# Causal attention in a macaron block: units of 32 queries with all sixteen heads for the maxima, the diagonal mask inside the product of the maxima, one summed tile for each query block

## The chip, the core and the metric

The kernel runs on one core of a Trainium2 chip. The metric is the device time of one launch in microseconds; the time before is the median of three runs. The engines are called PE (TensorE matmul), PEld (its weight loads), DVE (VectorE), ACT (ScalarE), POOL (GpSimd) and SP (SyncE, which here issues nearly all transfers).

## What is computed

The input x is 16 x 512 x 128 (batch elements, tokens, width), fp32. A feed-forward half step, causal attention and another feed-forward half step follow each other, each on a normalised input:

```python
x = x + 0.5 * ffn(layernorm(x))
x = x + attn(layernorm(x))
x = x + 0.5 * ffn(layernorm(x))

# ffn: w = simulate_quantize_int4(kernel)
#      x @ w + bias + (x @ a) @ b                      128 -> 128, rank 16
# attn, 16 heads of 64, latent of 32:
#      q = x Wq ; lat = x Wkv_down ; k = lat Wk_up ; v = lat Wv_up
#      attn = softmax(where(key <= query, q k / 8, lowest)) ; y = attn v ; y Wout
```

The kernel folds Wk_up into Wq and Wv_up into Wout, so that a head's query has 32 entries (LD) and keys and values are the latent itself, the same 32 rows for all heads.

## The kernel before

Scores are computed twice for each batch element. The first time queries lie on the partitions and keys along the free axis (`sx`, `s_parts`); DVE reduces them to the negated row maximum (`find_maxima`, L651 and L655, tile `nmax`). The second time keys lie on the partitions and queries along the free axis (`tx`, `t_parts`), the negated maximum is added by a small product, and ACT takes the exponential (`exponentials`, L664) into the probabilities `pt`. These are the moving operand of the product with the latent (`values`, tile `o`, L763) and of the product with ones for the row sums (`sums`, tile `s`, L763). All four groups of 32 partitions hold a copy of the 32 latent rows, one for each of four heads, so PE runs four products side by side, one on each group of 32 rows of its array (scores) or of 32 columns (values, sums, queries, projection).

The sixteen heads form four groups of four (`HG`, `NG`). Work goes through pairs of groups. A pair takes five steps, in each of which every head streams 512 score columns:

```python
STEP = ((0, 0), (1, 0), (2, 0), (1, 1), (0, 1))
T_BLOCKS = (((0, 0, 512, 0),), ((3, 384, 128, 0), (1, 128, 384, P)))
```

Kind 0 is query block 3 against all four key blocks for the maxima, and key block 0 against all queries for the probabilities; kind 1 joins query blocks 2 and 0 (key blocks 3 and 1); kind 2 is query block 1 (key block 2) for both groups of the pair. A batch element takes ten steps, the sixteen of them 160, n = 0 to 159.

In a step, `burst(n, s_at, t_at)` issues the score products of step n and the probability products of the step LAG = 6 earlier. `merge` (L641) interleaves the two streams of matmuls on PE. The maxima need the causal mask on the diagonal blocks: for each of four sub-blocks of 32 queries a bf16 product of `mask_w` and `eye2_b` adds -1e30 above the diagonal. The small product that brings the maxima takes them as three bf16 terms (`maxima`, L728 to L732 on POOL; turned by PE in `maxima_t`, tile `mt`; stored by ACT as `rows`), with `ones_u` as weights. It does not mask; after the exponential POOL zeroes the upper triangles of `pt` (`zeros`, L677).

For the row sums POOL first adds probability tiles of equal query range (`add_01`, L747; `add_2`, L752; `add_23`, L757), and PE then multiplies ones with three tiles of 128, 384 and 128 columns (`sum_products`). The sums go to DRAM one head at a time (L799), come back over 128 partitions (L801), DVE takes the reciprocal (L831), and this goes through DRAM again and is broadcast to the 32 partitions of each head (L833, L836, tile `rb`). POOL multiplies values and reciprocals (`normalise`, L839, tile `ot`), and PE projects (`yp`, L385).

Between the bursts stands the gap: values, sums, turned maxima of earlier steps, and parts of other batch elements. `plan` puts the parts of `front` (first feed-forward, normalisation, keys `kt_ps`, queries `qt_ps`) and `tail` (projection, second feed-forward `fp_c`) at fixed steps given by tuples such as FRONT_STEPS and TAIL_STEPS. Each engine runs its instructions in the order in which they are issued here; SP issues the transfers, in the same order. The reciprocal square root of the normalisation is refined by one Newton step of three DVE instructions on 12 columns (`ln_newton`, L344 to L346). Before step 0 the weights are prepared; after step 159 `late_burst` and the code behind it work off the six probability steps that remain.

The PSUM banks are two pools: four single banks (`bank`, for `tx` and the products in the gaps) and two pairs (`two_banks`, for `sx` and at times a third product of a gap).

Of the kernel before, what the change touches and what calls it, by code (L numbers as in the profile page):

```python
# [11 lines left out]
F32 = mybir.dt.float32  # L12
# [6 lines left out]
P = 128  # L19
# [6 lines left out]
def macaron_kernel(  # L26
# [24 lines left out]
    assert D == P and NT * P == L and L <= 512 and HG == 4 and H % HG == 0  # L51
    scale = HD**-0.5
# [4 lines left out]
    io = ctx.enter_context(tc.tile_pool(name="io", bufs=3))  # L57
# [54 lines left out]
    def load_heads(src, n, name):  # L112
        t = const.tile([P, NW, n], F32, tag=name, name=name)
        nc.sync.dma_start(t, src.rearrange("(t p) n -> p t n", p=P))
        return t

    wq_sb = load_heads(wq_t, D, "wq_sb")
    wk_sb = load_heads(wk_t, LD, "wk_sb")
    xs[1] = load_x(1)
    zs[1] = load_blocks(x[1], "a1")  # L120
    wv_sb = load_heads(wv_t, LD, "wv_sb")
    wo_sb = load_heads(wout, D, "wo_sb")
# [8 lines left out]
    terms = []  # L131
    for k in range(2):
        t3 = const.tile([P, NT, P], BF16, tag=f"terms{k}", name=f"terms{k}")
        nc.vector.memset(t3, 0.0)
        terms.append(t3)
    ones_u = const.tile([P, 2, P], BF16, tag="ones_u", name="ones_u")
# [6 lines left out]
    eye_b = const.tile([P, LD], BF16, tag="eye_b", name="eye_b")  # L143
    for h in range(HG):
        rows = slice(h * LD, (h + 1) * LD)
        nc.vector.tensor_copy(eye_b[rows, :], ident[rows, ts(h, LD)])
    eye2_b = const.tile([P, 2, LD], BF16, tag="eye2_b", name="eye2_b")
    for k in range(2):
        nc.vector.tensor_copy(eye2_b[:, k, :], eye_b)
    for u in range(2):  # L150
        pick = const.tile([P, 1], F32, tag=f"pick{u}", name=f"pick{u}")
        nc.vector.tensor_reduce(pick, ident.rearrange("p (h c) -> p c h", c=LD)[:, 3 * u : 3 * u + 3, :], AX.XY, ALU.max)
        nc.vector.tensor_scalar(ones_u[:, u, :], ones_f, pick, None, ALU.mult)


    mask_w = const.tile([P, NT, P], BF16, tag="mask_w", name="mask_w")
    nc.gpsimd.memset(mask_w, 0.0)

    def masks():
        for h in range(HG):  # L160
            rows = slice(h * LD, (h + 1) * LD)
            nc.gpsimd.affine_select(
                mask_w[rows, :, :], mask_w[rows, :, :], pattern=[[-LD, NT], [1, P]],
                compare_op=ALU.is_ge, fill=MASK, base=0, channel_multiplier=-1,
            )
# [175 lines left out]
    def ln_newton(ln, whats):  # L341

        y, e, r, var = columns(ln, whats)
        nc.vector.scalar_tensor_tensor(e, var, EPS, y, ALU.add, ALU.mult)  # L344
        nc.vector.scalar_tensor_tensor(e, e, -0.5, y, ALU.mult, ALU.mult)
        nc.vector.scalar_tensor_tensor(r, e, 1.5, y, ALU.add, ALU.mult)  # L346
# [4 lines left out]
    def ln_scale(src, name, ln):  # L351

        xn = act2.tile([P, NT, D], F32, tag="xn", name=f"xn_{name}")
        for t in range(NT):
            nc.scalar.activation(xn[:, t, :], src[:, t, :], AF.Copy, scale=rstd(ln, "b", t))  # L355
        return xn
# [7 lines left out]
    def turn_blocks(z, name, tag):  # L364
        xt = act2.tile([P, L], F32, tag=tag, name=f"{tag}_{name}")
        nc.vector.transpose(xt, z.rearrange("p n c -> p (n c)"))
        return xt

    def turn(src, name, tag):
# [3 lines left out]
        xt = act2.tile([P, L], F32, tag=tag, name=f"{tag}_{name}")  # L373
# [3 lines left out]
    def with_bias(src, name, engine):  # L377
        xb = act2.tile([P, NT, D], F32, tag="xb", name=f"xb_{name}")
# [10 lines left out]
    def ffn(xt, ln, xb, name, tag, bufs):  # L389


        return ffn_out(ffn_product(xt, name), ln, xb, name, tag, bufs)

# [6 lines left out]
    def ffn_out(fp, ln, xb, name, tag, bufs):  # L400
        dst = io.tile([P, NT, D], F32, tag=tag, name=f"{tag}_{name}", bufs=bufs)
# [16 lines left out]
    def normalised(w):  # L418
        whats = [k for k, b in (("c", w - 2), ("b", w + 2), ("a", w + 3)) if 0 <= b < (B - 2 if k == "c" else B)]
# [4 lines left out]
        ln_newton(lns[w], whats)  # L424
        yield

    def front(b, st):
# [23 lines left out]
        x1 = st["x1"] = ffn(xt, la, xb, na, "x1", 5)  # L451
# [11 lines left out]
        xnt = turn_blocks(z, nb, "xnt_b") if b else turn(xn, nb, "xnt_b")  # L463
        yield
        mp = take(f"kt_ps_{b}")
        kt = st["kt"] = act2.tile([P, L], F32, tag="kt", name=f"kt_{b}", bufs=3)
# [21 lines left out]
        def query(g):  # L488
            mp = take(f"qt_ps_{b}_{g}")
            product(mp, wqk_flat[:, ts(g, P)], xnt)  # L490
            if g % 2 == 0:
                st["qt", g] = act2.tile([P, 2, L], F32, tag="qt", name=f"qt_{b}_{g}", bufs=4)
            nc.scalar.copy(st["qt", g - g % 2][:, g % 2, :], mp)  # L493

        yield
        query(0)
        yield
        query(1)
        yield
        query(2)  # L500
        yield
        query(3)
        yield

    def latent(b, st):

        lat = st["lat"] = act2.tile([P, NT, LD], F32, tag="lat", name=f"lat_{b}", bufs=3)
# [7 lines left out]
    FRONT_STEPS = (-31, -30.5, -29, -28, -21, -19.25, -16, -16, -13, -10.5, -8, -4.25, -4, -3.5, -3.25, -2, 3, 4)  # L515
    SECOND_STEPS = (-9.5, -8.5, -7, -5.5, -5, -4.25, -4, -3.5, -3.25, -2, 3, 4)
    THIRD_STEPS = (-18.5, -18.5, -18.5, -18, -17.5, -17.25, -16, -16) + FRONT_STEPS[8:]
    FOURTH_STEPS = (-27, -26, -25.5, -25) + FRONT_STEPS[4:]
    TAIL_STEPS = (1.75, 2.5, 2.75, 3.5, 4.5, 7, 7, 7.75, 10.5)
    NORMALISED_STEPS = (5, 6)  # L520

    def tail(b, st, late=False):


        x2 = io.tile([P, NT, D], F32, tag="x2", name=f"x2_{b}")
        nm = f"c{b}"
        ln = ln_tile(nm) if late else ln_of("c", b)
        for half in (0, 1):
            yp = take(f"yp_{b}_{half}")[:, : 2 * D]
            for t in (0, 1):  # L530
                for g in range(NG):
                    product(yp[:, ts(t, D)], st["ot"][:, g, ts(2 * half + t, P)], wvo[:, g, :],
                            t == 0 and g == 0, g == NG - 1)
            nc.vector.tensor_tensor(
                x2[:, ts(half, 2), :], yp.rearrange("p (t d) -> p t d", d=D), st["x1"][:, ts(half, 2), :], ALU.add
            )
            if half and not late:
                there = to_dram(x2, nm)
            yield
            ln_stats(x2, ln, "c", (2 * half, 2 * half + 1))  # L540
            yield
        if late:
            ln_rstd(ln, "c")
            yield
            ln_newton(ln, "c")
            yield
            xt = turn(x2, nm, "xt_c")
        else:
            z = load_blocks(there, nm)
            yield  # L550
        xb = with_bias(x2, nm, nc.vector if late else nc.gpsimd)
        yield
        if not late:
            xt = turn_blocks(z, nm, "xt_c")
            yield
        fp = ffn_product(xt, nm)
        if late:
            yield
        x3 = ffn_out(fp, ln, xb, nm, "x3", 3)
        if not late:  # L560
            yield
# [4 lines left out]

    STEP = ((0, 0), (1, 0), (2, 0), (1, 1), (0, 1))

# [539 lines left out]
```

## Time and profile before

| what | value |
|---|---|
| runs | 810.03, 811.99, 812.89 us; median 811.99 |
| profiled execution | span 808.8 us (no separate time is listed for it) |
| PE | busy 786.1 us (97%), 15400 matmuls |
| PE weight loads | 507.6 us (63%) |
| POOL | 676.1 us (84%), 675 instructions |
| DVE | 620.9 us (77%), 1318 |
| ACT | 488.1 us (60%), 971 |
| mean granted TensorE clock | 0.995 |
| first score product, first probability product, last step's end | 30.28, 52.35, 767.76 us |
| chain that ended last | PE 70%, DVE 9%, POOL 6%, DMA 5%, ACT 5% |

A product in fp32 appears as two matmul instructions. The busy time of a group is the union of its instructions, so it is less than count times mean where four run side by side. A matmul's duration includes the time in which it drains, and so overlaps the next one's start; the time of a section on PE is better taken from its start to the next section's start. The steady part repeats every batch element, ten steps.

### The profile page before, as it was taken

To read this page: it belongs to the slowest core of one execution; us is meant where nothing else is said; L and a number is where in the kernel's file an instruction comes from. 1 tells how busy PE (TensorE), PEld (TensorE's weight loads), DVE (VectorE), ACT (ScalarE), POOL (GpSimd) and SP (SyncE) were. 2 spreads that over 40 slices of the span, in tenths; PEclk is the share of its full clock that TensorE was granted. 3 is DMA by queue.
4 is the path that set the end of the run, shared out by engine and by line. 5 is a ranking of instruction groups with operands and counts; after the bars stand their busy time and mean duration, and the time that the engine had idled before them with its cause. 6 is when DMAs were issued, how large, how long until landed. Compare 5 with 4: busy or idle time off the path is not lost.

```text
span 808.8 us, 35715 instructions
## 1 busy us (share of the span) xinstructions
PE 786.1 (97%) x15400; PEld 507.6 (63%) x15400; DVE 620.9 (77%) x1318; ACT 488.1 (60%) x971; POOL 676.1 (84%) x675
## 2 busy tenths in 40 slices
PE   7899999999999999999999999999999999999987
PEld 5556566675666667666666666666566666666644
DVE  7887886878878697877869787777978777686817
ACT  1237675657566675756657575666657666665661
POOL 1018989999988999989899898989989979998992
PEclk9989999999999999999999999999999999999999
DMA  5123122232422323332232423223223222211201
GB/s 138 28 57 68 32 69 68 65 72 73 95 61 70 80 62 83 74 83 60 70 89 55 93 63 82 69 61 93 51 53 77 58 63 66 70 44 47 58 24 48
DMA packets 171022, 54.01 MB, mean 67 GB/s; under 512 B 119512, under 2 KB 162680, under 8 KB 170864
## 3 DMA queue, kind: packets, MB, share of 16 engines
q1 hardware_dynamic: 170096, 51.44, 27.2%
q8 instruction: 120, 1.97, 1.0%
q10 hardware_dynamic: 768, 0.30, 0.1%
q14 instruction: 38, 0.31, 0.1%
HBM read 37.90 MB, written 13.80 MB: 64 GB/s over the span
## 4 chain that ended last, share of the span: by engine, by line
PE 70%; DVE 9%; POOL 6%; DMA 5%; ACT 5%; SPq 2%; issue 2%; DVEq 0%; POOLq 0%; ACTq 0%
PE sx L641 17%; PE o L763 14%; PE tx L641 13%; PE s L763 7%; PE qt_ps L385 6%; PE yp L385 6%; DVE nmax L651 3%; POOL b L747 3%; DMA rb<-recs 2%; PE fp_c L385 2%; ACT xn_b L355 2%; DMA recs<-rec 2%; PE fp_a L385 1%; POOL ot L839 1%; ACT pt L664 1%
## 5 line engine op out<-in xcount | busy, mean ns | idle before, releaser
L651 DVE TENSOR_REDUCE nmax<-sx 128x2 f32<-128x768 f32 (+2 forms) x384 | 312.6, 863 | 105.9 <-PE tx L641 67.6
L664 ACT ACTIVATE pt<-tx 128x512 f32<-128x512 f32 x616 | 319.5, 598 | 85.3 <-PE tx L641 78.8
L641 PE MATMUL sx<-kt,qt 32*128 32x512 f32 (+3 forms) x2048 | 324.4, 444 | 0.0
L641 PE MATMUL tx<-qt,kt 32*128 32x512 f32 x1728 | 319.3, 469 | 0.0
L747 POOL TENSOR_TENSOR b<-pt,pt 128x768 f32<-128x768 f32 x126 | 226.8, 1822 | 0.5
L641 PEld LDWEIGHTS sx<-kt,qt 32*128 32x128 f32 x2048 | 176.8, 186 | 24.7 <-issue 1.0
L677 POOL TENSOR_SCALAR_AFFINE_SELECT pt<-pt 128x1024 f32<-128x1024 f32 (+1 forms) x162 | 144.8, 900 | 17.2 <-ACT pt L664 15.4
L763 PE MATMUL o<-pt,lat 128*32 128x512 f32 x1984 | 146.4, 435 | 0.8 <-POOL pt L677 0.8
L641 PEld LDWEIGHTS tx<-qt,kt 32*128 32x128 f32 x1728 | 131.5, 185 | 5.1
L763 PEld LDWEIGHTS o<-pt,lat 128*32 128x32 f32 x1984 | 62.5, 109 | 77.9 <-issue 59.0
L641 PE MATMUL tx<-rows,ones_u 6*128 6x512 bf16 (+1 forms) x988 | 109.9, 297 | 1.1 <-DVE wvo L292 0.5
L839 POOL TENSOR_TENSOR ot<-osb,rb 128x512 f32<-128x512 f32 x62 | 79.0, 1275 | 35.9 <-DMA rb<-recs 33.6
L655 DVE TENSOR_REDUCE nmax<-sx 128x4 f32<-128x1024 f32 x64 | 75.4, 1219 | 31.9 <-PE tx L641 31.8
L782 ACT COPY osb<-o 128x512 f32<-128x512 f32 x62 | 36.3, 585 | 92.1 <-PE o L763 92.1
L641 PE MATMUL sx<-eye_b,mask_w 32*128 32x64 bf16 (+1 forms) x2560 | 87.8, 183 | 2.4 <-DVE nmax L655 1.7
L641 PEld LDWEIGHTS <-ones_u 6*128 6x128 bf16 x1024 | 43.1, 92 | 74.3 <-issue 61.6
L641 PEld LDWEIGHTS <-mask_w 32*128 32x128 bf16 x2560 | 67.4, 92 | 32.7 <-issue 24.6
L752 POOL TENSOR_TENSOR b<-b,pt 128x512 f32<-128x512 f32 x63 | 80.5, 1278 | 5.1
L757 POOL TENSOR_TENSOR b<-pt,pt 128x512 f32<-128x512 f32 x63 | 80.4, 1276 | 0.1
L385 PE MATMUL qt_ps<-xnt_b_b,wqk 128*32 128x512 f32 x512 | 68.0, 603 | 0.2
L763 PE MATMUL s<-b,ones_f 128*32 128x384 f32 x992 | 65.1, 380 | 3.1 <-POOL b L752 2.6
L493 ACT COPY qt<-qt_ps 128x512 f32<-128x512 f32 x64 | 37.5, 586 | 48.4 <-PE qt_ps L385 48.4
(194 smaller groups left out, 815.6 us busy)
## 6 DMA issues: line engine op xcount, KB each, us to landing
rb<-recs SPq DMA_DIRECT2D x248, 64.0 KB
x<-in_x_dram SPq DMA_DIRECT2D x16, 256.0 KB
sums<-ssb SPq DMA_DIRECT2D x248, 2.0 KB
z_a<-in_x_dram SPq DMA_DIRECT2D x60, 64.0 KB
blocks_b<-xn_b SPq DMA_DIRECT2D x15, 256.0 KB
z_b<-blocks_b SPq DMA_DIRECT2D x60, 64.0 KB
kt<-kt_d SPq DMA_DIRECT2D x60, 64.0 KB
out_dram<-x_c SPq DMA_DIRECT2D x15, 256.0 KB
```

The costliest lines, as they stand in the source:

```text
L385: nc.tensor.matmul(dst[ts(h, LD), :], lhsT=w[:, ts(h, LD)], rhs=mv, start=start, stop=stop, skip_group_check=True)
L493: nc.scalar.copy(st["qt", g - g % 2][:, g % 2, :], mp)
L641: nc.tensor.matmul(dst, lhsT=w, rhs=mv, start=first, stop=last, skip_group_check=True)
L651: nc.vector.tensor_reduce(nmax[:, i, heads, u], sx[:, :, col : col + (i + 1) * P], AX.X, ALU.max, negate=True)
L655: nc.vector.tensor_reduce(nmax[:, 1, heads, :], sx.rearrange("p k (u n) -> p k u n", u=2), AX.X, ALU.max, negate=True)
L664: nc.scalar.activation(pt[:, :, 2 * pair + k, :], tx[k].rearrange("p (b n) -> p b n", n=P), AF.Exp)
L677: nc.gpsimd.affine_select(diag, diag, pattern=[[0, diag.shape[1]], [1, P]], compare_op=ALU.is_ge, fill=0.0, base=0, channel_multiplier=-1,)
L747: nc.gpsimd.tensor_tensor(*flat, ALU.add)
L752: nc.gpsimd.tensor_tensor(b01, b01, st["pt", 2, g][:, u], ALU.add)
L757: nc.gpsimd.tensor_tensor(both, st["pt", 2, g][:, 2 + u], st["pt", 1, g + u][:, 0], ALU.add)
L763: nc.tensor.matmul(dst[ts(h, LD), :].rearrange("p (b n) -> p b n", n=P), lhsT=w[h] if isinstance(w, list) else w, rhs=mv, start=start, sto ...
L839: nc.gpsimd.tensor_tensor(turned(st)[:, g, :], st["osb", g], st["rb", g], ALU.mult)
```

## The change

The scores of a query are taken for all sixteen heads at once. `qt` now holds, for each of the four partition groups, query and head group interleaved (`(q g)`: 512 queries x 4 groups), so that 128 columns of it are 32 queries of four groups.

* For the maxima a unit is one or two blocks of 32 queries (`S_UNITS`), and a block's product ends at its own last key: block qb streams (qb + 1) x 32 key columns. The mask is one small product for each head and unit (`tri`, 32 columns wide, `eye4`).
* For the probabilities a unit is one pair of query block i and key block j <= i of 128 each (`T_UNITS`, ten pairs), 512 columns of (query, group) for each of the four partition groups.
* On the diagonal pairs the product of the maxima carries the mask as well. The turned maxima have 32 rows for each partition group, three of them the bf16 terms and 26 a one-hot of the query; the weights `diag_w` hold -1e30 for masked pairs. 128 queries are cut into five pieces of 26 (`SUB`, `SUBS`), so five small products of up to 104 columns stand in place of one of 512. `zeros` is gone.
* `nmax` is split into bf16 terms and turned three times an element instead of twice.
* For the row sums POOL adds whole tiles of 2048 columns (`add`, six an element) until one tile for each query block is left; PE multiplies ones with that one tile. Sums and reciprocals travel for two query blocks at a time: one transfer out, one back, one out, four broadcasts.
* Values of block i are i + 1 products of 512 columns. The copies of `qt`, `o` and `s` by ACT interleave or separate query and group.
* The Newton step of the planned normalisations runs on POOL as five instructions.
* LAG is 5. All four query products of the first element precede step 0, and the planned parts, the gaps and the end are laid out anew. Weights and a helper tile share the six `pt` buffers; several tiles have other buffer counts.

```diff
-    STEP = ((0, 0), (1, 0), (2, 0), (1, 1), (0, 1))
-    T_BLOCKS = (((0, 0, 512, 0),), ((3, 384, 128, 0), (1, 128, 384, P)))
+    S_UNITS = ((12,), (13,), (14,), (15,), (8, 3), (9, 2), (10, 1), (11, 0), (7, 4), (6, 5))
+    T_UNITS = ((3, 0), (3, 1), (3, 2), (3, 3), (2, 0), (2, 1), (2, 2), (0, 0), (1, 0), (1, 1))
...
+    def s_parts(sc, st, unit, pair, masks_last):
...
-        for s in range(NT):
-            for k in range(2):
-                rows = ts(2 * pair + k, LD)
-                small_.append((diag[:, k, :, ts(s, LD)], mask_w[rows, s, :],
-                               eye2_b[rows, : diag.shape[2], :], not masks_last and s == 0, masks_last))
...
+                small_.append((at, eye4[rows], tri[rows, : len(ends), :], not masks_last and m == 0, masks_last))
+        for n_, qb in enumerate(unit):
+            w, col = both[n_]
             for k in range(2):
                 rows = ts(2 * pair + k, LD)
+                large.append((sc[:, k, col : col + w], st["qt"][rows, ts(qb, P)], st["kt"][rows, :w],
+                              masks_last and n_ == 0, not masks_last))
...
+    def t_parts(tx, st, unit, pair, maxima_last=False):
+        i, j = unit
...
+            if i == j:
+                for m in range(SUBS):
+                    q = slice(m * SUB * NG, min((m + 1) * SUB, P) * NG)
+                    up = slice(r * LD, r * LD + LD)
+                    small_.append((tx[k][:, q], diag_w[up, int(i == 0), m, :], top[up, q], first and m == 0, maxima_last))
             else:
+                up = slice(r * LD, r * LD + 3)
+                small_.append((tx[k], ones_b[up, :], top[up], first, maxima_last))
+            large.append((tx[k], st["kt"][rows, ts(j, P)], st["qt"][rows, ts(i, L)], maxima_last, first))
...
-    def zeros(st, g, kind, u, heads=slice(0, 4)):
-        pt = st["pt", kind, g + (u if kind < 2 else 0)]
-        diag = pt[:, : (1 if kind == 0 else 2), heads].rearrange("p b k n -> p (b k) n")
-        nc.gpsimd.affine_select(
...
+    def add(st, i, one, two):
+        left, right = st["pt", i, one], st["pt", i, two]
+        if ("both", i, one) not in st:
+            st["both", i, one] = probs.tile([P, HG, L], F32, tag="both", name=f"both_{st['b']}_{i}{one}", bufs=3)
...
+        nc.gpsimd.tensor_tensor(st["both", i, one], left, right, ALU.add)
...
+    def values(st, i):
+        o_ps = take(f"o_{st['b']}_{i}")
+        for j in range(i + 1):
+            streamed(o_ps, st["lat"][:, j, :], st["pt", i, j], j == 0)
...
+        for k, w in enumerate(which):
+            s_ps = take(f"s_{b}_{w}")
+            streamed(s_ps, ones_f[:, :LD], st.get(("both", w, 0), st["pt", w, 0]), True)
+            nc.scalar.copy(*by_group(ssb[:, ts(k, L)], s_ps))
...
+    def ln_newton(ln, whats, engine):
+        if engine is nc.gpsimd:
+            engine.tensor_scalar(e, var, EPS, -0.5, ALU.add, ALU.mult)
+            engine.tensor_tensor(r, y, y, ALU.mult)
+            engine.tensor_tensor(e, e, r, ALU.mult)
+            engine.tensor_scalar(e, e, 1.5, None, ALU.add)
+            engine.tensor_tensor(r, e, y, ALU.mult)
...
+    FRONT_STEPS = (-28, -27, -26, -20, -19, -18, -17, -16.5, -11, -9.5, -7.5, -6.25, -6, -5)
+    QUERY_STEPS = (-5, -4, -3, -2)
+    TAIL_STEPS = (0, 1, 2, 3, 3.5, 5, 6, 7, 9)
+    NORMALISED_STEPS = (4, 4.5)
...
+    STEPS, LAG = len(S_UNITS), 5
...
+    GAPS = {
+        0: ((maxima_t, 2, 1),),
+        2: ((values, 2, 1),),
+        3: ((sums, (3, 0), 1), (values, 0, 1)),
+        4: ((maxima_t, 0, 0),),
+        5: ((values, 1, 1),),
+        6: ((sums, (2, 1), 1),),
+        8: ((maxima_t, 1, 0),),
+        9: ((values, 3, 0),),
+    }
+    RECIPROCALS = {5: (((3, 0), 1),), 8: (((2, 1), 1),)}
+    NORMALISED = {7: ((3, 1), (0, 1)), 9: ((2, 1), (1, 1))}
+    ADDED = {
+        7: ((3, 0, 1, 0),),
+        9: ((3, 2, 3, 0),),
+        0: ((3, 0, 2, 1),),
+        1: ((2, 0, 1, 1),),
+        3: ((2, 0, 2, 1),),
+        5: ((1, 0, 1, 1),),
+    }
+    TERMS = {3: 0, 7: 1, 9: 2}
```

In these tables the key is the step within an element, and the last number of an entry says how many elements back its work belongs. In a step POOL's instructions are issued in the order: add, split of the maxima (TERMS), products with the reciprocals (NORMALISED).

## The prediction

> **What bounds the kernel now.** The first view read was the windows view, busy time of each engine in stretches of one batch element (columns: stretch, length, then busy time and instructions of PE, PEld, DVE, ACT, POOL; granted clock, DMA share, GB/s):
>
> ```profile
> 463.36:510.30 46.94, 46.79 (x954) 30.36 (x953) 37.38 (x78) 30.13 (x61) 42.74 (x43) 1.00 0.31 71
> 510.30:557.34 47.04, 46.80 (x955) 30.36 (x953) 36.72 (x78) 30.15 (x61) 42.79 (x43) 1.00 0.33 76
> ```
>
> An element takes 47.0 us, PE is busy through all but 0.2 us of it at full clock, and POOL is second with 42.8. So the price of an edit is PE time, as long as POOL stays below PE. The next view is PE's timeline inside that element. It shows one burst, from 513.45 to 515.68, and two sections behind it:
>
> ```profile
> 513.45 0.39 PE L641 MATMUL tx<-rows,ones_u 6*128 6x512 bf16 x2
> 513.46 0.26 PE L641 MATMUL sx<-eye_b,mask_w 32*128 32x32 bf16 x8
> ...
> 515.40 0.25 PE L641 MATMUL sx<-eye_b,mask_w 32*128 32x32 bf16 x8
> 515.68 0.43 PE L763 MATMUL s<-pt,ones_f 128*32 128x128 f32 x8
> 515.93 1.05 PE L763 MATMUL s<-b,ones_f 128*32 128x384 f32 x16
> 516.79 0.41 PE L385 MATMUL mt<-ident_b,terms 128*32 128x128 bf16 x16
> 517.13 0.70 PE L641 MATMUL tx<-qt,kt 32*128 32x512 f32 x2
> ```
>
> Taking each section from its start to the next one's start, the element 510.30 to 557.34 is: ten bursts 22.65, values (o) 9.04, sums (s) 4.96, queries (qt_ps) 3.79, projection (yp) 3.54, the two feed-forward products 1.80, turned maxima (mt) 0.68, keys 0.39, idle 0.19; together 47.04. One of the four sums takes 1.54 instead of 1.11, and the chain of waits names what holds it:
>
> ```profile
> 544.13 3.55 POOL b L747 x2
> 547.69 0.07 issue
> 547.75 1.29 POOL b L752
> 549.04 0.04 issue
> 549.09 1.07 PE s L763 x16
> ```
>
> Last came the groups by form (busy time, mean ns of one), for the prices:
>
> ```profile
> L747 POOL TENSOR_TENSOR b<-pt,pt 128x768 f32<-128x768 f32 x126 | 226.8, 1822 | 0.5
> L651 DVE TENSOR_REDUCE nmax<-sx 128x2 f32<-128x1024 f32 x128 | 152.7, 1219 | 43.7 <-PE tx L641 42.1 <-PE sx L641 1.0
> L752 POOL TENSOR_TENSOR b<-b,pt 128x512 f32<-128x512 f32 x63 | 80.5, 1278 | 5.1
> L651 DVE TENSOR_REDUCE nmax<-sx 128x2 f32<-128x256 f32 x128 | 53.1, 415 | 0.0
> L345 DVE SCALAR_TENSOR_TENSOR e_w<-e_w,y_w 128x12 f32<-128x12 f32 x11 | 17.4, 1580 | 0.4
> L346 DVE SCALAR_TENSOR_TENSOR r_w<-e_w,y_w 128x12 f32<-128x12 f32 x11 | 4.4, 399 | 0.4
> ```
>
> **PE, part by part, per element.** Both kernels have ten steps an element.
>
> Score columns. Before, every row group streams 10 x 512 = 5120 columns for the maxima. After, the units are 416, 448, 480, 512 and six of 416 columns, 4352: 768 fewer. The values section prices a column, with four matmuls side by side: 9.04 us for 5120 columns, 1.77 ns; the sums give 1.11 us for 640, 1.73 ns. That is -1.3 us.
>
> Mask matmuls. A row group has 4 in a burst, then 1 (2560 to 640 in all). In the start-up, where no other work is mixed in, eight of them in two row groups hold the next product back by 0.12 us, 30 ns each:
>
> ```profile
> 32.82 0.29 PE L641 MATMUL sx<-eye_b,mask_w 32*128 32x64 bf16 x8 [0.26 <-DVE nmax L651]
> 32.94 1.12 PE L641 MATMUL sx<-kt,qt 32*128 32x384 f32 x8
> ```
>
> Three fewer by 0.03 by ten bursts is -0.9. The upper bound is the 0.28 us from 515.40 to 515.68: three quarters of it would be -2.1, but most of that time is the last products draining ahead of a section of another shape, which stays. I take -0.9.
>
> Sums. One stream of 512 columns in place of 128+384+128 = 640: 4 x 128 x 1.73 ns, rounded down for the start of each section, -0.75 (bounds -0.6 and -0.9).
>
> Values: the same columns in 10 streams instead of 16; between nothing and -0.3, I take -0.1.
>
> Turned maxima: three instead of two, one takes 517.13 - 516.79 = 0.34, so +0.34.
>
> Diagonal key blocks. Four of the ten probability units replace one 512-column small product for each head by five of 104 columns or fewer: 16 more matmuls for a row group. Columns are the same, so the lower bound is nothing. The upper bound is an unhidden weight load each: the loads of ones_u have a mean of 92 ns, 16 x 0.092 = +1.5. The nearest row is the masks', spaced at 30 ns, less than the 47 ns that 104 columns stream (512 take 0.23 us, 513.45 to 513.68). I take +0.2.
>
> Narrow score products. Three for a row group have 96, 64 and 32 columns, fewer than any before. A 32x128 fp32 load takes a mean of 186 ns, so three unhidden pairs bound it at about +0.8, none at 0; before, 128-column products beside a 512-column stream show no gap. I take +0.2.
>
> The wait on POOL in the sums (0.43) goes, since the last add of a query block is queued one to three steps ahead of its sums. A new one of the same order comes after the step with only keys and turned maxima behind it (0.39 + 0.34 us): two exponentials of 0.52 us each follow a burst before its last banks are free, so the next burst starts up to 0.4 late. I set one against the other.
>
> Sum: -1.3 - 0.9 - 0.75 - 0.1 + 0.34 + 0.2 + 0.2 = -2.3. The element goes from 47.0 to 44.7.
>
> **The cover: does another engine reach 44.7?** POOL first. Removed: the zeroing, 162 x 0.900 / 16 elements = 9.1, and the adds, 4 x (2 x 1.822 + 1.278 + 1.276) = 24.8. Added: six adds of 2048 columns. From 768 at 1.822 and 512 at 1.277, a column costs 2.13 ns and an instruction 0.19 us, so one is 4.55, six 27.3. Beside them 4 products with the reciprocals at 1.275 = 5.1, two biases 2.5, three sets of maxima splits at 1.5 (512.01 to 513.47) = 4.5, and the Newton step moved here as five small instructions, 1.5. Together 40.9, against 42.8 now. The order matters as well. The longest unbroken stretch runs from the landing of rb for blocks 2 and 1 over two products, an add, a bias, two adds and the split to the turned maxima: 2.55 + 4.55 + 1.27 + 9.1 + 1.5 = 19.0. In front of it lie 18 us of PE steps up to the reciprocal and some 6 us of DMA (rec ends at 536.4, rb is used at 542.85, 6.4 later; another took 5.3). About 43 against 44.7: it fits, with little to spare.
>
> DVE: the reduces. 1024 columns 1.219 and 256 columns 0.415 give 1.05 ns a column and 0.15 for an instruction. Before 20,480 columns in 28 instructions, 25.6; after 17,408 in 32, 23.0. The Newton step takes 2.8 more off (L344 to L346: 0.81 + 1.58 + 0.40). 37 becomes 31.6, no bound. ACT has the same forty exponentials and one copy more, 30.7. Its qt, osb and ssb copies get a stride of 16 bytes, for which no row exists; were each doubled from 0.585 that is 12 x 0.585 = 7, still 37.7. SP issues 14 transfers an element for sums and reciprocals instead of 40.
>
> [...]
>
> [...]
>
> **Span.** Before: first product of the probabilities at 52.35, last step ends at 767.76, span 808.8: 52.35 + 715.4 (154 steps) + 41.0. After: the middle scaled by 44.7/47.0 is 680.4, and since the probabilities follow 5 steps behind instead of 6, one step more runs mixed, +4.4. Start: three query products move ahead of the first step (+2.8) and some 3 us of DVE work for the diagonal masks stands before the first reduce, but only four steps' reduces, not five, must pass before the first maxima are turned (-2.4), and the reduces are shorter (-0.9, and -1 for small DVE work dropped at the start): 52.35 + 1.5 = 53.9, between 50 and 56. End: one burst alone fewer (1.2) and one DMA round trip of sums less, against longer adds: 41.0 - 3 = 38, between 35 and 43. Sum 53.9 + 684.8 + 38 = 776.7. The median of the runs, 811.99, is 3.2 above the profiled span (no separate time is listed for that execution): 780.
>
> **Rivals.**
> Slower: POOL sets the pace. Its place is the stretch of 19.0 above; each us by which the adds or rb come late past 1.7 us of slack is one us an element, some 15 us in all. It beats the gain from 4 us on, with adds of 5.9 us (three of them lie in it) or rb landing after 10 us, not 6. For it: the transfers of rb double to 128 KB each, and 33.6 us of waits for rb stand before L839 already. Against: the adds are linear in two rows. At 48 us an element: 730.6 + 4.8 + 53.9 + 40 + 3.2 = 832.
> Half of that: POOL's idle 4.2 us an element stays as it is and a little is added, 45.9: 698.7 + 4.6 + 53.9 + 38 + 3.2 = 798.
> Faster still: the mask matmuls are worth their upper bound and the small pieces cost nothing, 43.1: 656.0 + 4.3 + 53.9 + 38 + 3.2 = 755.
>
> **How the numbers follow.** Forecast 0.42 (its own range 768 to 792), faster still 0.24, half held by POOL 0.20, POOL-bound 0.12, and 0.02 for a sum of misses that ends within 0.3%, about what a measurement of this kernel can tell from no change. Hence faster 0.86, same 0.02, slower 0.12. The range 750 to 806 leaves out the slower case and the far end of the fast one.
>
> **What would show it.** Right: elements of 44 to 45.5 us in the windows view, PE busy all through, POOL adds near 4.55 us, about 640 mask matmuls, bursts of 2.0 to 2.1 us. Wrong: PE waiting on POOL terms or b before mt or s (POOL-bound); bursts on diagonal blocks 0.3 longer than the others (weight loads); strided ACT copies above 0.6 us; a start of the probabilities past 56 us.

## The result, and the profile after

The changed kernel takes 836.01 us (median of four runs, 834.44 to 837.16); the kernel before, run beside it, 811.26. The ratio is 1.030, interval 1.028 to 1.033: slower, where 780 us was forecast. The profiled execution has a span of 833.2 us and a time of 834.96.

The same split of the span as in the forecast shows where the 56 us between forecast and result lie. The first product of the probabilities comes at 57.51 (forecast 53.9), the last step of both kinds ends at 791.16, 733.65 later (forecast 684.8), and 42.0 follow (forecast 38). So 48.9 of the 56 us are in the middle, 3.6 at the start, 4.0 at the end, and -0.4 in the distance of the runs from the span.

The windows view, one batch element (columns as before: stretch, length, then busy time and instructions of PE, PEld, DVE, ACT, POOL; granted clock, DMA share, GB/s):

```profile
459.45:507.48 48.03, 46.98 (x745) 24.87 (x745) 32.03 (x76) 32.73 (x62) 39.43 (x33) 1.00 0.30 71
```

48.0 us instead of the forecast 44.7, at full clock. POOL is busy for 39.4 (forecast 40.9) and further from the end than before; DVE's 32.0 is close to the 31.6 of the forecast. No engine but PE is near the length of the element, and PE's 46.98 of busy time has stalls in it. The next view shows one. It is PE's timeline in the burst from 491.67 to 494.11 (start, length, line, output and inputs, shapes):

```profile
491.67 0.39 PE L648 MATMUL tx<-rows,ones_b 3*128 3x512 bf16 x2
...
492.33 0.59 PE L648 MATMUL tx<-qt,kt 32*128 32x512 f32 x2
...
492.56 0.76 PE L648 MATMUL tx<-rows,ones_b 3*128 3x512 bf16 x2
...
492.95 0.69 PE L648 MATMUL tx<-qt,kt 32*128 32x512 f32 x1
```

A burst writes four `tx` banks, two and two. The pair of small products at 491.67 takes 0.39 us; the same pair for the second half, at 492.56, takes 0.76: its second matmul was late. ACT's timeline names the reason: the query copy that empties one of the four banks runs until 492.90.

```profile
490.95 0.58 ACT L752 COPY osb<-o 128x512 f32<-128x512 f32 x1 [0.60 <-PE o L738]
491.81 1.09 ACT L528 COPY qt<-qt_ps 128x512 f32<-128x512 f32 x1 [0.27 <-PE qt_ps L422]
```

The groups of POOL's adds, of the copies of `o` and of the query copies on the page (busy time, mean ns of one | idle before):

```profile
L733 POOL TENSOR_TENSOR both<-pt,pt 128x2048 f32<-128x2048 f32 x63 | 286.8, 4553 | 19.5 <-ACT pt L670 19.5
...
L752 ACT COPY osb<-o 128x512 f32<-128x512 f32 x61 | 35.7, 585 | 77.3 <-PE o L738 75.0
L528 ACT COPY qt<-qt_ps 128x512 f32<-128x512 f32 x64 | 70.0, 1111 | 10.0 <-PE qt_ps L422 9.7
```

A query copy takes 1111 ns. Before the change the page had:

```profile
L493 ACT COPY qt<-qt_ps 128x512 f32<-128x512 f32 x64 | 37.5, 586 | 48.4 <-PE qt_ps L385 48.4
```

The new copy writes every fourth word, 16 bytes apart. The copy of `o`, which reads PSUM 16 bytes apart and writes in one run, takes 585 ns as before. The adds take the 4.55 us of the forecast.

The chain of waits shows two more places. The first is the step from which the element is counted; ACT's queue holds four normalisations `xn_b` between the copy of `o` and the exponentials, and PE stands until these are done:

```profile
463.21 0.59 ACT osb L752
463.80 1.17 ACT xn_b L392 x4
464.97 0.97 ACT pt L670 x2
```

The second is the burst before the values of block 3, which follows a gap of query product and turned maxima, 1.2 us long:

```profile
503.74 1.06 ACT pt L670 x2
504.80 0.48 ACT rows L722
505.28 1.00 ACT qt L528
506.28 0.04 issue
506.32 0.58 PE tx L648 x4
```

Last, the waits of PE's weight loads put down two groups to DVE, which empties the banks of the two feed-forward products (columns: us in total, times, longest):

```profile
PEld L648 <- DVE x L434: 9.4, 13, 0.7
PEld L648 <- DVE xb_c L434: 8.4, 14, 0.7
```

Before, the first feed-forward product (`fp_a`) stood ahead of the values in its gap; after, it stands behind them, directly ahead of the burst. So five gaps of ten now end with one of these products: `fp_a`, `fp_c`, and three query products (ahead of s6, s7 and s9 of the table below) whose copies take twice as long. In the element of before three gaps ended with a query product, none with a feed-forward product.

### The profile page after: what moved, and what is told of

It is laid out like the page before. It is cut to its first block, busy times and chain, and to the rows that moved or that the text cites. A ratio compares the mean times of both kernels' runs of the same rounds, so it can differ in the third digit from the quotient of the medians.

```text
span 833.2 us, 28263 instructions
## 1 busy us (share of the span) xinstructions
PE 786.0 (94%) x12068; PEld 421.4 (51%) x12068; DVE 544.2 (65%) x1302; ACT 530.3 (64%) x996; POOL 632.0 (76%) x537
## 4 chain that ended last, share of the span: by engine, by line
PE 71%; ACT 11%; POOL 6%; DVE 6%; DMA 3%; issue 2%; SPq 1%; DVEq 0%; POOLq 0%; ACTq 0%
PE tx L648 21%; PE o L738 14%; PE sx L648 12%; PE yp L422 7%; PE s L738 7%; ACT pt L670 6%; PE qt_ps L422 5%; POOL both L733 3%; POOL ot L783 2%; DVE nmax L660 2%; DMA rb<-recs 2%; PE fp_a L422 2%; ACT xn_b L392 2%; PE fp_c L422 1%; ACT qt L528 1%
## 5 line engine op out<-in xcount | busy, mean ns | idle before, releaser
L660 DVE TENSOR_REDUCE nmax<-sx 128x2 f32<-128x256 f32 (+15 forms) x512 | 345.9, 717 | 177.0 <-PE tx L648 85.8
L648 PE MATMUL sx<-kt,qt 32*128 32x416 f32 (+15 forms) x2048 | 312.4, 420 | 0.5 <-ACT qt L528 0.5
L733 POOL TENSOR_TENSOR both<-pt,pt 128x2048 f32<-128x2048 f32 x63 | 286.8, 4553 | 19.5 <-ACT pt L670 19.5
L648 PE MATMUL tx<-rows,ones_b 3*128 3x512 bf16 x384 | 81.2, 382 | 7.0 <-ACT qt L528 3.5
L528 ACT COPY qt<-qt_ps 128x512 f32<-128x512 f32 x64 | 70.0, 1111 | 10.0 <-PE qt_ps L422 9.7
L733 POOL TENSOR_TENSOR both<-both,both 128x2048 f32<-128x2048 f32 x16 | 72.7, 4541 | 0.0
L733 POOL TENSOR_TENSOR both<-both,pt 128x2048 f32<-128x2048 f32 x15 | 68.2, 4545 | 1.2
L648 PE MATMUL sx<-tri,eye 32*128 32x64 bf16 (+1 forms) x640 | 62.1, 188 | 5.0 <-DVE nmax L660 5.0
L422 PE MATMUL yp<-wvo,ot 128*32 128x128 f32 x1920 | 59.6, 277 | 5.7 <-POOL ot L783 4.0
L422 PEld LDWEIGHTS yp<-wvo,ot 128*32 128x32 f32 x1920 | 51.8, 111 | 15.2 <-ACT pt L670 6.8
L648 PE MATMUL tx<-rows,diag_w 32*128 32x104 bf16 (+1 forms) x1280 | 54.5, 205 | 2.3 <-ACT osb L752 0.6
```

Of the source, the lines that this page charges most:

```text
L422: nc.tensor.matmul(dst[ts(h, LD), :], lhsT=w[:, ts(h, LD)], rhs=mv, start=start, stop=stop, skip_group_check=True)
L528: nc.scalar.copy(qt.rearrange("p (q g) -> p g q", g=NG)[:, g, :], mp)
L648: nc.tensor.matmul(dst, lhsT=w, rhs=mv, start=first, stop=last, skip_group_check=True)
L660: nc.vector.tensor_reduce(st["nmax"][:, slot(qb), ts(pair, 2)], sx[:, :, col : col + w], AX.X, ALU.max, negate=True)
L733: nc.gpsimd.tensor_tensor(st["both", i, one], left, right, ALU.add)
```

## The experiments

The table gives all ten bursts of an element, from start of the burst to start of what follows, for the changed kernel and most variants, each from an element in the middle of its profile. s0 is the burst behind the values of block 3.

| kernel | element us | s0 | s1 | s2 | s3 | s4 | s5 | s6 | s7 | s8 | s9 |
|---|---|---|---|---|---|---|---|---|---|---|---|
| changed kernel | 48.01 | 2.48 | 2.13 | 2.18 | 2.55 | 2.21 | 2.66 | 2.44 | 2.30 | 2.64 | 2.64 |
| dense query copies | 46.92 | 2.48 | 2.12 | 2.18 | 2.54 | 2.21 | 2.68 | 2.06 | 2.09 | 2.64 | 2.13 |
| queries first in the gap | 47.48 | 2.47 | 2.13 | 2.18 | 2.55 | 2.21 | 2.67 | 2.06 | 2.08 | 2.64 | 2.67 |
| feed-forward first in the gap | 47.14 | 2.48 | 2.13 | 2.18 | 2.16 | 2.08 | 2.52 | 2.44 | 2.31 | 2.52 | 2.64 |
| xn_b ahead of the values | 47.46 | 2.00 | 2.12 | 2.18 | 2.55 | 2.21 | 2.66 | 2.44 | 2.30 | 2.64 | 2.63 |
| query copies on DVE | 48.35 | 2.48 | 2.12 | 2.18 | 2.55 | 2.21 | 2.66 | 2.44 | 2.31 | 2.80 | 2.45 |
| order mended | 46.04 | 1.99 | 2.13 | 2.17 | 2.16 | 2.08 | 2.53 | 2.06 | 2.08 | 2.51 | 2.67 |
| order mended, dense copies | 45.27 | 1.99 | 2.13 | 2.18 | 2.15 | 2.08 | 2.53 | 2.06 | 2.08 | 2.08 | 2.33 |
| order mended, query 0 moved | 45.59 | 2.00 | 2.13 | 2.18 | 2.16 | 2.08 | 2.23 | 2.06 | 2.09 | 2.51 | 2.67 |
| order mended, query 0 moved, dense copies | 44.67 | 1.99 | 2.13 | 2.18 | 2.16 | 2.08 | 2.09 | 2.06 | 2.08 | 2.07 | 2.33 |

The values of 2.47 and 2.48 in the column s0 hold 0.41 of idle time. Most elements of a run agree within a few hundredths, single ones are 0.1 to 0.4 longer; the runs with copies on DVE vary more.

### Dense query copies

```diff
-            nc.scalar.copy(qt.rearrange("p (q g) -> p g q", g=NG)[:, g, :], mp)
+            nc.scalar.copy(qt[:, ts(g, L)], mp)
```

> The four query copies of an element write their 512 columns densely, group after group, instead of every fourth column; every other instruction is the same, and the queries then stand in the wrong order, so the values computed are not the reference's. Theory A (bursts wait for PSUM banks that the gap's products still hold, because ACT takes 1.11 us for a strided query copy): the copy falls to 0.59 us, the bursts after a gap with a query, 2.44, 2.31 and 2.63 us long in the steady element, fall to 2.1 to 2.2, the element from 48.0 to about 47.0, the run by 14 to 18 us from 836. Theory B (POOL's adds set the pace): no change beyond 2 us. Theory C (the bursts are long of themselves, by narrow score products and by weight loads on the diagonal): no change beyond 2 us.

822.26 us, ratio 1.014 to the kernel before (1.011 to 1.017). The group of the copies on this run's page:

```profile
L528 ACT COPY qt<-qt_ps 128x512 f32<-128x512 f32 x64 | 38.5, 602 | 11.0 <-PE qt_ps L422 11.0
```

The same copy with a dense target is back at 602 ns, so it is the stride of the write that doubles it. s6, s7 and s9 fall by 0.38, 0.21 and 0.51, the three bursts that have a query product in the gap before them and not as its first part. They make up the 1.1 us an element. The bursts s0, s3, s5 and s8 stay: the stride is a third of the loss, and no more.

### Queries first in the gap

```diff
-    QUERY_STEPS = (-5, -4, -3, -2)
+    QUERY_STEPS = (-5.25, -4.25, -3.25, -2.25)
```

> The query product is issued as the first product of its gap instead of the last, so it takes the bank whose next use comes later, and its copy runs beside the product behind it. Nothing else moves. Theory A: the bursts behind these gaps (2.44, 2.63 us) fall to about 2.1, the element by 0.8 to 1.1 us, the run by 12 to 17 us from 836. Theory B and theory C: no change beyond 2 us, since neither the amount of work nor the adds change.

829.45 us, ratio 1.022 (1.020 to 1.024). s6 and s7 fall as with the dense copy, with the stride still there: with sums or values behind it in the gap the long copy is hidden (2.06 and 2.08 us). s9 does not fall (2.67). What it waits for has changed, in the waits of PE:

```profile
PE tx L648 <- ACT rows L722: 5.0, 14, 0.4
```

In the gap of 1.2 us the query copy now stands ahead of the copy of the turned maxima in ACT's queue, and that one comes late instead. Order alone did not mend this gap, which is shorter than the two copies in it (0.48 and 1.00 us in the changed kernel's chain).

### Feed-forward products first in the gap

```diff
-    FRONT_STEPS = (-28, -27, -26, -20, -19, -18, -17, ...
+    FRONT_STEPS = (-28, -27, -26, -20, -19, -18.25, -17, ...
-    TAIL_STEPS = (0, 1, 2, 3, 3.5, 5, 6, 7, 9)
+    TAIL_STEPS = (0, 1, 2, 3, 3.5, 5, 6, 6.75, 9)
```

> The two feed-forward products of an element are issued as the first product of their gaps, ahead of values or query, so that the four DVE instructions that empty their bank (1.13 us) end earlier. Theory A: the burst of step 3 falls from 2.55 to about 2.15 us and that of step 8 from 2.64 to 2.3 (its second bank is then held by a query copy), the element by 0.6 to 0.9, the run by 9 to 13 us from 836. Theories B and C: no change beyond 2 us.

826.74 us, ratio 1.019 (1.016 to 1.021). s3 falls by 0.39, s4, s5 and s8 by 0.12 to 0.14; 0.3 had been expected of s8, which a query copy still holds. The bank that DVE empties was a second, separate cause, and it has nothing to do with the layout of `qt`.

### One-input copies in place of POOL's adds

```diff
-        nc.gpsimd.tensor_tensor(st["both", i, one], left, right, ALU.add)
+        nc.gpsimd.tensor_copy(st["both", i, one], right)
```

> Each of the six adds of an element on POOL becomes a copy of its second input, so the row sums leave out most of their terms; every dependence stays. POOL's 27.3 us of adds should fall to about half. Theory B: the element falls with POOL, towards 45 us or less, the run by 40 us or more. Theory A: POOL idles 8.6 of 48 us already and ends in time; the steady element stays within 0.3 us, and only the end of the kernel, where two adds stand in the chain, gains, 3 to 6 us in all.

837.44 us, ratio 1.031 (1.027 to 1.036), as the changed kernel. Page and windows view of this run:

```profile
L733 POOL COPY both<-pt 128x2048 f32<-128x2048 f32 x78 | 147.6, 1892 | 79.8 <-ACT pt L670 79.8
```

```profile
459.47:507.52 48.05, 46.94 (x745) 24.85 (x744) 32.00 (x76) 32.74 (x62) 23.52 (x32) 1.00 0.31 71
```

POOL has 16 us an element less to do, and the element keeps its 48.05 us. The slower rival of the forecast, POOL setting the pace at 832 us, named a time near the measured one by a mechanism that is not there. The gain of 3 to 6 us that theory A expected at the end does not show in the time of the run; its end is taken up further below.

### Normalisation ahead of the values; a start-up cast on ACT

```diff
-    FRONT_STEPS = (..., -17, -16.5, -11, -9.5, ...)
+    FRONT_STEPS = (..., -17, -16.5, -11.25, -9.5, ...)
...
-            nc.vector.tensor_copy(
+            nc.scalar.copy(
                 eye4[rows], ident[rows, ts(h, LD)].unsqueeze(2).to_broadcast([LD, LD, NG])
             )
```

> Two edits at places that do not touch. The four ACT instructions that scale the normalised input (xn_b) are issued ahead of values of block 3 instead of behind them; and the four casts that build the mask's eye4 at the start run on ACT, which is idle there, instead of DVE. Theory A: in step 0 of each element the exponentials no longer queue behind the scaling, the 0.41 and 0.17 us of PE idle around the turned maxima go, 0.5 to 0.6 us an element, 8 to 9 us in all. Start: theory D says that the casts took 4.2 us on DVE because POOL's mask instructions shut them out; on ACT the first weight product starts 2 to 3 us earlier than 12.8. Together 836 falls by 10 to 12 us. A rival for the start (the chain waits for the weights' transfers, not for DVE) has the first weight product stay at 12.8.

828.04 us, ratio 1.020 (1.017 to 1.022): 8 us gained where 10 to 12 were expected. s0 falls from 2.48 to 2.00, and the element by 0.55. The second edit is about the start. The timeline of the changed kernel there, DVE and POOL:

```profile
4.14 4.19 DVE L162 CAST eye<-ident 32x128 bf16<-32x128 f32 x4
4.21 5.42 POOL L174 TENSOR_SCALAR_AFFINE_SELECT diag_w<-diag_w 32x1280 bf16<-32x1280 bf16 x4
```

Four casts of 128 columns take 4.19 us beside POOL's four selects. In this experiment ACT makes them:

```profile
4.49 1.21 ACT L162 CAST eye<-ident 32x128 bf16<-32x128 f32 x4 [2.42 <-POOL tri L158]
```

1.21 us, beside the same selects. The products of the weights (`wqk_ps`), which wait for a maximum that DVE takes behind these casts (PE waits 4.5 us for it in the changed kernel), start at 8.25 instead of 12.74, and the first product of the probabilities at 55.96 instead of 57.51. Other DVE steps stay long at that place: the cast to `ident_b` takes 1.10 us where the kernel before has 0.31. So the first weight product starts 4.5 us earlier and the first product of the probabilities only 1.6; what holds the rest was not taken apart.

One by one in the changed kernel's timeline, the first cast starts 0.07 us before the first select and takes 0.21 us; the other three take 1.25, 1.35 and 1.35 and end at 5.61, 6.97 and 8.33, each 0.08 behind the end of a select (5.53, 6.89 and 8.25). These ends agree with theory D; by what the casts are held was not shown, and no run here has these four on DVE without the selects.

### Query copies on DVE

```diff
-            nc.scalar.copy(qt.rearrange("p (q g) -> p g q", g=NG)[:, g, :], mp)
+            nc.vector.tensor_copy(qt.rearrange("p (q g) -> p g q", g=NG)[:, g, :], mp)
```

> The strided query copies run on DVE instead of ACT; the output is the reference's. What a strided copy costs on DVE no row shows; dense it is 0.69 us. If DVE pays nothing for the stride, theory A expects the same gain as with dense copies on ACT, 12 to 16 us off 836, perhaps more, since ACT also loses four copies an element. If DVE pays double as ACT does (1.4 us), the gain is half of that or less. Theory C expects no change.

842.36 us, ratio 1.038 (1.036 to 1.040), slower than the changed kernel. From the page:

```profile
L528 DVE COPY qt<-qt_ps 128x512 f32<-128x512 f32 x64 | 69.2, 1094 | 36.2 <-PE qt_ps L422 35.6
```

A strided copy takes on DVE what it takes on ACT; the one dense copy of this size that DVE makes out of PSUM (`kt`, L501 of the changed kernel) takes 691 ns. DVE's queue holds the reduces as well (up to 512 columns of two heads at a time). ACT makes no query copy in this run, and s6 and s7 stay at 2.44 and 2.31: these two wait for the bank and not for ACT's queue. s9 falls by 0.19, so there ACT's queue has a part. The element in the table has 0.35 of waiting in its sums; most elements take 48.0 to 48.2, three 48.4 to 49.1. Of the 9.0 us by which the profiled span is longer than the changed kernel's, 2.8 lie at the start, 2.1 in the middle and 4.1 at the end.

A second experiment with this copy on DVE and the order mended (feed-forward first, `xn_b` ahead, the cast on ACT) shows no gain from DVE's copies either:

> All of it together: feed-forward products first in their gaps, query copies on DVE, the scaling ahead of values, eye4 on ACT. If the gains add: 14 (queries) + 9 (feed-forward) + 8.5 (scaling) + 2.5 (start) = 34 us off 836, that is 802, ahead of the kernel before by about 1%. If a stall that is taken away only uncovers the next one, less: 810 to 820.

828.26 us, ratio 1.020 (1.017 to 1.023), element 47.0. s0 and s3 fall to 2.00 and 2.16; s6 to s9 stay at 2.3 to 2.85. The gains did not add, and the time is above both of the expected values.

### The order mended, copies on ACT

```diff
-    FRONT_STEPS = (-28, -27, -26, -20, -19, -18, -17, -16.5, -11, ...)
-    QUERY_STEPS = (-5, -4, -3, -2)
-    TAIL_STEPS = (0, 1, 2, 3, 3.5, 5, 6, 7, 9)
+    FRONT_STEPS = (-28, -27, -26, -20, -19, -18.25, -17, -16.5, -11.25, ...)
+    QUERY_STEPS = (-5.25, -4.25, -3, -2.25)
+    TAIL_STEPS = (0, 1, 2, 3, 3.5, 5, 6, 6.75, 9)
```

The start-up cast is on ACT here and in all that follows.

> The same, but with the query copies on ACT at 1.11 us and the query product first in its gap where values, sums or turned maxima follow. Queries first gave 6.6 us alone, so 6.6 + 9 + 8.5 + 2.5 = 27 us off 836, 809. It should stay 5 to 10 us behind the version with DVE copies if ACT's queue is what the banks wait for.

809.56 us (median of ten runs), ratio 0.998 (0.996 to 0.999). Six numbers of the order and one cast take 26 us off the changed kernel and bring it to the time of the kernel before. The sum of the single gains held (809 expected). The comparison with the copies on DVE did not: this kernel was expected 5 to 10 us behind that one and is 18.7 ahead. s5, s8 and s9 are left at 2.5 to 2.7.

Three more runs start from this kernel. The first has dense copies, the second moves query 0, the third splits a copy between two engines.

> The changed kernel with the four placements mended (809.6 us, element 46.0), and the query copies also written dense: the queries then stand in the wrong order, so the output is not the reference's; the time shows what the stride still costs once the order is mended. Theory (the bank held twice as long by the strided write is what the probability products still wait for): the step with the 0.36 wait for the rows copy behind a query copy goes, element 45.4 to 45.7, time 801 to 805. Rival (order alone mattered, the stride is now covered): within 2 us of 809.6.

800.99 us, ratio 0.989 (0.986 to 0.992). Where the theory had s9 alone, s8 falls as well (2.51 to 2.08), s9 to 2.33; together 0.77 an element.

```diff
-    QUERY_STEPS = (-5.25, -4.25, -3, -2.25)
+    QUERY_STEPS = (-6, -4.25, -3, -2.25)
```

> The same mended kernel with query 0 moved into the gap that had only the keys and the turned maxima behind the burst (0.95 us long). Theory (my own wait term: a gap shorter than the two exponentials behind a burst makes the next burst late; before this the burst after it took 2.53 against 2.1): that burst falls to 2.1 to 2.2, the gap that loses query 0 still has 1.9 us of other products, element 45.6, time 802 to 804. Rival (that burst is late for another reason, or the copy put there takes the place of the short gap): no change, 808 to 811, with the next burst held by the query copy of 1.1 us on ACT.

801.58 us (median of six), ratio 0.989 (0.987 to 0.992), element 45.59: as the theory has it. s5 falls from 2.53 to 2.23, and the wait in front of the turned maxima goes with it. Of the kernels that keep the whole computation this is the fastest, 34 us below the changed kernel and 1.1% below the kernel before.

```diff
-            nc.scalar.copy(qt.rearrange("p (q g) -> p g q", g=NG)[:, g, :], mp)
+            to = qt.rearrange("p (q g) -> p g q", g=NG)[:, g, :]
+            nc.scalar.copy(to[:, : L // 2], mp[:, : L // 2])
+            nc.vector.tensor_copy(to[:, L // 2 :], mp[:, L // 2 :])
```

> The same mended kernel with each query copy split in halves of 256 columns, one on ACT and one on DVE, both with the stride, output as the reference's. Theory (what matters is how long the copy holds its bank and its engine's queue): each half about 0.6 us, as long as the dense copy was, and 2 us an element off ACT; element 45.5 to 45.8, time 802 to 806. Rival (DVE's half waits behind the reduces of 1.2 us, so the bank is held as long as before): 808 to 814.

818.04 us, ratio 1.008 (1.005 to 1.011): slower than unsplit. The waits of DVE, and those of PE:

```profile
DVE qt L530 <- ACT qt L529: 27.3, 63, 0.9
```

```profile
PE yp L422 <- POOL ot L785: 11.0, 8, 4.9
```

The halves did not run side by side: DVE's waited for ACT's in 63 of 64 cases, so that the bank was held for both halves, 648 and 631 ns at the median. A shorter hold was therefore not tested. In six of fifteen elements the time is 46.0 to 46.3, as unsplit; in six it is 46.8 to 47.6 (the first one and the last two are shorter, as in every run), where the projection waits for POOL's products, these for reciprocals that land late (one such wait of POOL takes 2.06 us). Why they land late with more work in DVE's queue was not followed further.

### The order mended, query 0 moved, dense copies

The kernel with query 0 moved, and dense copies besides:

> The mended kernel with query 0 moved (801.6 us, element 45.6) and the query copies dense besides: the queries stand in the wrong order, so the output is not the reference's; the time shows what the working of the forecast gives when no query copy holds a bank longer than the copies of the kernel before did. Theory (the forecast's terms for PE were right and only stalls were missed): the two bursts that still take 2.5 and 2.7 fall to 2.1 to 2.3, element 44.8 to 45.1, time 790 to 795. Rival (some 0.5 us of the terms themselves, small pieces or narrow products, was missed too): element 45.3 or more, time 797 to 801.

790.03 us, ratio 0.976 (0.974 to 0.978). The windows view of this run:

```profile
431.91:476.58 44.67, 44.51 (x746) 24.60 (x745) 31.92 (x77) 30.30 (x62) 39.21 (x33) 1.00 0.33 77
```

The element takes 44.67 us, where the forecast had 44.7. All bursts but one lie between 1.99 and 2.18; s9, at 2.33, has some 0.25 of a stall left. The run is still 10.1 us above the forecast's 779.9: 2.2 at the start (first product of the probabilities at 56.09), 4.3 in the middle (689.1, to 745.22), 4.8 at the end (42.8) and -1.2 in the distance of the runs from the span. These were not taken apart.

## Why the prediction was wrong

**The terms for PE's work were right in sum.** Score columns, masks, sums, values, turned maxima and small products sum to 44.3 without any wait, and to 44.7 with the 0.4 that the forecast allowed for a new one. The last experiment changes none of these terms and gives 44.67, of which some 0.25 is the stall in s9: 44.4 against 44.3. That 44.67 is the very 44.7 of the forecast is luck in part, since that number had another wait in it. Term by term the misses are up to 0.3 and nearly cancel. The bursts sum to 21.2, where the forecast's terms give 22.65 - 1.3 - 0.9 + 0.2 + 0.2 = 20.85; values take 9.10 (8.94), sums 3.57 (3.78), turned maxima 1.07 (1.02) and the projection, which had no term, 3.77 (3.54). How the bursts divide into masks, pieces and narrow products no run separates. The 640 mask matmuls and the 4.55 us adds are there; the forecast's two bounds for unhidden weight loads (+1.5 and +0.8) are not reached.

**The step that failed is the wait term**: "The wait on POOL in the sums (0.43) goes ... A new one of the same order comes ... I set one against the other". The old wait did go. The new ones are not 0.4 but 48.0 - 44.3 = 3.7 us an element. The place that the forecast named, the short gap of keys and turned maxima, is one of them (s5); the run with query 0 moved puts it at 46.04 - 45.59 = 0.45, so this one was sized right. What it left out is that the same mechanism acts at every burst: a burst needs four `tx` banks, and the last product of the gap before it, whatever it is, must be emptied first. The runs give the others, taken off the changed kernel one at a time: `fp_a` and `fp_c` directly ahead of a burst 0.87; `xn_b` ahead of the exponentials in ACT's queue 0.55; the query copies with their stride 1.09. These with the short gap are 2.96; all together took 3.34 off, so 0.4 appears only in combination (s8, which both `fp_c` and a query copy hold). The 0.4 between 3.34 and 3.7 is the stall left in s9 and the misses of the terms. Nothing in the forecast went through the gaps of the new order with the question of what stands last in each and who empties it, though the diff shows that order (FRONT_STEPS, QUERY_STEPS, GAPS), and the bursts of the kernel before, 2.23 to 2.25 behind the three gaps that end with a query product, showed only that copies of 0.586 fit there.

**The cover of ACT was counted in the wrong unit.** The forecast saw that a stride of 16 bytes had no row, doubled the copies, and found 37.7 busy us of 44.7: covered. The doubling is right for the query copies (1111 ns) and wrong for the two kinds that read PSUM with the stride (585 ns). ACT's busy time was never the limit (32.7 measured). What the longer copy takes is the time for which a bank is not free, and that had no cover at all where the bank was the next one the burst writes: in the burst shown above the copy ended at 492.90, and the pair of small products took 0.76 us instead of 0.39.

**Start and end.** The start was 3.6 late of 53.9, outside the bounds of 50 and 56. The forecast has no term for the start-up's new selects on POOL (5.42 us) and new casts on DVE (4.19 us) side by side. The products of the weights began 3.4 us later than before (12.74 against 9.31), and this the forecast did not have. From there to the first score product it is 2.6 us more than before (2.8 for the queries in the forecast), and from there to the first product of the probabilities 0.8 less (the forecast's other terms come to 1.3 less). But the weights' delay is not all that holds the start: with the casts on ACT they begin earlier than before, at 8.25, and the first product of the probabilities still comes at 55.96. At the end, 42.0 lies within the bounds of 35 and 43; the chain names POOL's long adds there (4.5 us each). With copies in place of the adds the end is 40.1; the variants that keep the adds lie between 40.9 and 46.2, one profile each, so the price of the adds there stays open.

**A slip that carried no weight.** Three unhidden pairs of loads of 186 ns are 1.1 us and not 0.8; neither was reached.

**The rivals.** That POOL sets the pace falls with the adds shortened by 16 us an element for no gain. Half of it falls with the same run. The faster rival had an element of 43.1; with the stalls gone but for some 0.25 it is 44.67. The case that came true, many small waits for banks, was not among the rivals, and the 0.86 for faster rested on its absence.

## What to carry to other kernels

When a change lays out the work anew, go through each gap and ask which product stands last, which engine empties its bank, what is queued in front of that on this engine, and how long the gap is against it; a sum of removed work says what the kernel could take and not what it does. Here a copy's cost was the time for which its bank stayed occupied (1111 ns against 602, worth 1.09 us an element over four copies), not its share of ACT, which was busy for 32.7 of 48.0 us. In this kernel six numbers of the order and one cast were worth 34 us, 836.0 to 801.6, as much as the forecast had hoped for from the whole change.

## What the runs showed of the hardware

* Writing fp32 words 16 bytes apart into SBUF nearly doubled a copy of 512 columns out of PSUM on ACT, 586 to 1111 ns; on DVE the strided copy took 1094 ns, a dense one 691. 256 strided columns took 648 ns on ACT and 631 on DVE (medians). Reading PSUM with the same stride and writing in one run cost ACT nothing: 585 ns, as the copy of `o` took before the change.
* POOL copies 2048 columns in 1892 ns and adds two such tiles in 4553.
* Four DVE casts of 128 columns on 32 partitions took 4.19 us beside POOL's selects; ACT made the same four in 1.21 beside the same selects. Three of the four on DVE ended 0.08 us behind the end of a select.
* Small products of 104 columns with 128-column bf16 weights showed little cost for the weight loads (mean 92 ns in the changed kernel): in the last run, among bursts with 416 score columns, those with five pieces (s4, s8) take 2.07 and 2.08 us, the unstalled ones with one piece (s0, s5, s6, s7) 1.99 to 2.09.
